# Centring the key weights on VectorE and GpSimd, and placing the first stage's filler work by order

## The chip, the cores and the metric

The kernel runs on one core of a Trainium2 chip. A core has a matrix engine (TensorE, PE in the profile; its weight loads are listed apart as PEld), three engines for elementwise work (VectorE or DVE, ScalarE or ACT, GpSimd or POOL) and a queue that starts transfers from memory (SyncE or SP). Each engine works through its own list of instructions in order, and waits where an operand isn't there yet. The metric is the device time of one execution in microseconds (us); lower is better.

## The reference: what is computed

A transformer block on a query sequence x of 128 rows and 512 columns, with a context of 12,544 rows and 512 columns. Everything is float32.

1. x is normalised twice, and gives self-attention queries q, keys k and values v, and cross-attention queries qx. Before each projection the input is divided by a scale per column, rounded to an 8-bit float, and multiplied back. q, k and qx are normalised per head of 128 columns.
2. The context is projected by `w_kv_x` to keys kx (8 heads of 128) and values vx (8 heads of 128); kx is normalised per head:

```python
kvx = jnp.einsum('bsi,oi->bso', cond, w_kv_x)
kx, vx = jnp.split(kvx, 2, axis=-1)
kx = _ln(kx.reshape(b, sc, g, d), kxln_w, kxln_b)
xout = _gqa(qx, kx, vx)
```

3. Self-attention over the 128 rows (called core) and cross-attention over the 12,544 context rows are concatenated, rounded to 8 bits, projected and added to x.
4. A causal self-attention block and a mixture-of-experts layer follow.

The normalisation of kx subtracts the mean over the 128 columns of a head. As the projection is linear, this mean can be taken from the weights beforehand: if the 128 weights of a head and an input row have their mean subtracted, the keys come out centred. Only the division by the standard deviation is left for later.

## The kernel before, in words

**First stage** (`pre` pools, lines 407 to 618). x is loaded and normalised, and turned (transposed on TensorE). Twelve projections of 512 columns follow: four for qx (numbers 0 to 3), two for k (4, 5), two for v (6, 7), four for q (8 to 11). `begin` (line 456) issues the four matmuls of one projection and asks for a further block of weights by `load_ahead`; `end` (line 475) normalises its result. `norm_heads` (line 147) does that: statistics on DVE (bn_stats, bn_aggr; tile `mv`), three small steps on POOL for the reciprocal deviation (tile `rs`, lines 157 to 160), one on DVE for the shift (tile `nb4b`, line 162), four scalings on ACT (tile `pnn`, line 164). The result is transposed on TensorE (tile `ps_t`) and evicted by ACT (tiles `qraw`, `kT`, `qT`; line 472). The loop at line 516 ends projection i and begins projection i + 3. `quantised` (line 442) makes the rounded inputs on DVE. Sixteen narrow matmuls (`ps_b`, line 536) multiply each head's `qraw` by a bias column. Then four rounds of self-attention, `weights_of` and `heads_of`, end each with a product `ps_core` (line 606), which is added to `x1c`.

**Context products.** Keys and values of a chunk of 512 context rows are computed as a two by two block product with seven block multiplications in place of eight. `mix_tokens` (line 252) makes the mixed input blocks (tiles `mix`), `mix_weights` (line 275) the mixed weight blocks (tiles `wsum`, and parts of `wkv` in place). `unit` (line 287) is a generator with four steps that issue seven products (tiles `a_ps`, `b_ps`, `c_ps`), evicted by ACT (tiles `p`, `u`) and DVE (into `KT` and `V`). `k_unit` gives keys (matmul at line 327), `v_unit` values (matmul at line 346). A chunk needs two units of each, 56 matmuls of 256 columns for the keys and 28 of 512 columns for the values.

**Filler.** The values of chunk 0 don't depend on the centring, so their units are used as work for TensorE between the projections: `filler` holds the eight steps of both value units; `next(filler)` is written at two places of the loop's program text, and the rest is drained after the self-attention, where the scheduler places each matmul by what it finds free. The two key units of chunk 0 follow.

**Centring of the key weights** (lines 545 to 558). For each of the eight blocks of 512 columns (4 row blocks k, 2 halves h) and each of the four heads in it, ACT copies the 128 columns with the scale -1/128 and an accumulated sum (line 555, into `junk`, the sum into `wm`), and then adds that sum to the columns (line 558). `mix_weights` for the keys' half follows on DVE.

**Main loop** (line 780): for each of 25 chunks, `scores` per head group (`s_ps`, line 640; evicted by ACT times the keys' reciprocal deviation `krs`, line 645), maxima on DVE, exponentials on ACT, running sums on POOL (`ol`, line 730), `outputs` (`o_ps`, line 738), and between them the values of this chunk and the keys of the next. `mix_tokens` of the next chunk is asked for there, on POOL; the scheduler issues it up to a chunk earlier. `k_rstd` makes `krs` from the sums of squares: a narrow product (`v_ps`), an addition on DVE (`kve`) and a power on POOL (line 382).

**What sets the order.** The kernel is written against a scheduler which lays out each engine's list when the program is built. `tc.issue_after(x)` keeps an instruction from standing before x. The hardware then follows these lists.

Of the kernel before, what the change touches and what calls it, by code (L numbers as in the profile page):

```python
# [21 lines left out]
T = 12544  # L22
NH, G, D = 16, 8, 128
# [22 lines left out]
def block_kernel(  # L46
# [23 lines left out]
    nc = tc.nc  # L70
# [9 lines left out]
    HS = 2 * S  # L80


    colt = keep.tile([P, NCOL], F32, name="colt")
    nc.sync.dma_start(out=colt, in_=cols)
    sc = keep.tile([P, 6], F32, name="sc")
# [9 lines left out]

    def scl(name):
        return sc[:, scn(name)]

    x1c = keep.tile([S, H], F32, name="x1c")
    nc.sync.dma_start(out=x1c, in_=x)  # L100


    ident = keep.tile([P, P], F32, name="ident")
# [43 lines left out]
    def norm_heads(dst, src, sname):  # L147


        st = small.tile([P, 4, 6], F32, tag="st4", name="st4")  # L150
        mv = small.tile([P, 4, 2], F32, tag="mv4", name="mv4")
        for j in range(4):
            nc.vector.bn_stats(st[:, j, :], src[:, j * D : (j + 1) * D])
        for j in range(4):
            nc.vector.bn_aggr(mv[:, j, :], st[:, j, :])
        v = small.tile([P, 4], F32, tag="ve4", name="ve4")
        nc.gpsimd.tensor_scalar(v, mv[:, :, 1], sc2[:, scn(sname)], EPS, ALU.mult, ALU.add)
        r = small.tile([P, 4], F32, tag="rs4", name="rs4")
        nc.gpsimd.tensor_tensor(r, v, mhalf[:, :4], ALU.pow)
        pool = nc.gpsimd.tensor_scalar(r, r, scl(sname), None, ALU.mult)  # L160
        b = small.tile([P, 4], F32, tag="nb4b", name="nb4b")
        dve = nc.vector.scalar_tensor_tensor(b, mv[:, :, 0], -1.0, r, ALU.mult, ALU.mult)
        for j in range(4):
            act = nc.scalar.activation(
                dst[:, j * D : (j + 1) * D], src[:, j * D : (j + 1) * D], AF.Identity,
                bias=b[:, j : j + 1], scale=r[:, j : j + 1],
            )
        return pool.ins, dve.ins, act.ins

    def norm_rows(dst, src, twice=False):  # L170

# [217 lines left out]
    def parts(units):  # L389
        for u in units:  # L390
            yield from u

    def keys(c, others, pool, tag):

        sums = {}
        todo = parts(k_unit(c, u) for u in range(2))
        for i in range(8):
            next(todo)
            if i % 4 == 3:
                sums[i // 4] = k_sums(c, i // 4)  # L400
            if others:
                others(i)
            if i == 6:
                k_rstd(c, 0, sums.pop(0), pool, tag)
        return sums

    with tc.tile_pool(name="pre", bufs=2) as pre, tc.tile_pool(name="pre1", bufs=1) as pre1, tc.tile_pool(
# [86 lines left out]
            return end_norm(i, "wq", "qln_w", "qln_b", qTs[-1])  # L494

        names = ["qx_in"] * 4 + ["k_in"] * 2 + ["v_in"] * 2 + ["q_in"] * 4
        filler = parts(v_unit(0, v) for v in range(2))
        mix_steps = mix_tokens(0, nc.vector)
        xs["qx_in"], made = quantised("qx_in")
        with tc.issue_after(made), tc.issue_after(turned[0]):  # L500
# [15 lines left out]
        for i in range(12):  # L516
            last = end(i)
            if last is not None:
                pooled, normed, act = last
                if i == 1:  # L520
                    scaled = act
            if i < 2:
                for step in steps[i]:
                    step()
# [6 lines left out]
                    xs[nm], _ = quantised(nm)  # L531
            if i + 3 < 12:
                begin(names[i + 3])
            if i == 3:
                for h in range(NH):
                    nc.tensor.matmul(
                        psb[:, h : h + 1], lhsT=qraws[h // 4][:, h % 4, :], rhs=col("kxln_b"),
                        start=True, stop=True,
                    )
                qbw = pre1.tile([32, NH, 4], F32, name="qbw")  # L540
                for k in range(4):
                    nc.vector.tensor_copy(qbw[:, :, k], psb[32 * k : 32 * k + 32])
                for b in range(4):
                    nc.vector.tensor_copy(qb[32 * b : 32 * b + 32], qbw)
            if i == 7:


                for k in range(NK):
                    for h in range(2):
                        wm = small.tile([P, 4], F32, tag="wm", name="wm", bufs=8)  # L550
                        for g in range(4):
                            wk = wkv[:, k, h, g * D : (g + 1) * D]
                            junk = pre.tile([P, D], F32, tag="junk", name="junk", bufs=1)
                            with tc.issue_after(scaled):
                                nc.scalar.activation(
                                    junk, wk, AF.Copy, scale=-1.0 / D, accum_out=wm[:, g : g + 1]
                                )
                            nc.scalar.activation(wk, wk, AF.Identity, bias=wm[:, g : g + 1])
                for k in range(2):
                    for step in mix_weights(nc.vector, slice(0, H), k):  # L560
                        step()
        made = pooled

        def weights_of(i):
# [48 lines left out]
            heads_of(i, pe)  # L613
            pe = nxt

        for _ in filler:
            pass
        sums = keys(0, None, pps, "ps")

# [5 lines left out]
    with main:  # L625
# [154 lines left out]
        for c in range(NCH):  # L780
# [328 lines left out]
```

## Time and profile before

| | us |
|---|---|
| median of 3 runs | 2216.09 (2210.39 to 2217.72) |
| the profiled execution | 2217.69 |
| its span | 2215.9 |
| TensorE busy in the span | 2162.0 (98%) |
| DVE, POOL, ACT busy in the span | 1287.5, 1066.5, 919.7 |
| first projection starts | 13.95 |
| projection 8 starts | 56.48 |
| first ps_core starts | 95.63 |
| first s_ps starts | 141.34 |
| third o_ps of chunk 0 starts | 176.25 |

Busy time by stretch of the first stage and of chunk 0, in us:

| stretch | TensorE | DVE | ACT | POOL |
|---|---|---|---|---|
| 28.8 to 56.5 | 25.3 of 27.7 | 19.1 | 23.3 | 6.7 |
| 56.5 to 95.6 | 34.7 of 39.1 | 19.6 | 24.6 | 11.4 |
| 95.6 to 141.3 | 45.7 of 45.7 | 23.6 | 11.7 | 0.1 |
| 141.3 to 176.3 | 31.7 of 35.0 | 25.8 | 20.3 | 18.0 |

How to read the lines that follow: a row of the timeline has the start, the length, the engine, the line of the kernel, the operation, the tile written and the tiles read, the shape, and how many instructions were merged; in brackets stands how long the engine was idle before, and what ended that. A matmul in float32 appears as two records, so x8 is four matmuls. DVE is VectorE, ACT is ScalarE, POOL is GpSimd. The granted clock is TensorE's, 1.00 being full speed.

### The profile page before, as it was taken

Reading aid. Unit: us, or ns where it says so; the run is one execution under the profiler, and the core shown is the slowest. Engines: PE = TensorE matmul, PEld = TensorE weight load, DVE = VectorE, ACT = ScalarE, POOL = GpSimd, SP = SyncE. Lnnn points to the kernel's source line nnn. Section 1 sums busy time; section 2 is a strip of 40 time slices with the busy share of each in tenths; the row PEclk is TensorE's granted clock in tenths of the full one; section 3 lists DMA queues with packets and bytes.
Section 4 is the critical chain, followed back from the end, with each engine's and each line's share of the span. In section 5 each row is a group of like instructions: output and inputs, shape, how many; then the busy total and the mean of one; then the engine's idle time right before and its main releaser. Section 6 shows DMA issues by size and latency. Waiting matters only on the chain.

```text
span 2215.9 us, 23861 instructions
## 1 busy us (share of the span) xinstructions
PE 2162.0 (98%) x8660; PEld 1543.1 (70%) x8660; DVE 1287.5 (58%) x2394; ACT 919.7 (42%) x1782; POOL 1066.5 (48%) x1157
## 2 busy tenths in 40 slices
PE   8999999999999999999899999999999999997899
PEld 4477767776776777677676776677677767765554
DVE  7455675566567556656666567556755765674211
ACT  4544454444345434544344444434544443440111
POOL 2214654674475456446574476456546744650000
PEclk9999999999999999999999999999999999998799
DMA  8300000000000000000000000000000000026393
GB/s 309 114 20 1 20 19 1 20 20 19 1 20 20 1 20 20 10 1 20 19 20 20 1 20 19 1 20 20 19 1 20 20 18 2 1 100 233 114 285 118
DMA packets 71222, 95.49 MB, mean 43 GB/s; under 512 B 3136, under 2 KB 39488, under 8 KB 71104
## 3 DMA queue, kind: packets, MB, share of 16 engines
q1 hardware_dynamic: 71104, 93.97, 12.7%
q8 instruction: 68, 1.11, 0.2%
q14 instruction: 50, 0.41, 0.1%
HBM read 93.69 MB, written 0.26 MB: 42 GB/s over the span
## 4 chain that ended last, share of the span: by engine, by line
PE 89%; DVE 4%; POOL 2%; issue 2%; DMA 1%; ACT 1%; SPq 1%; POOLq 0%; ACTq 0%; DVEq 0%
PE a_ps L327 15%; PE o_ps L738 14%; PE s_ps L640 14%; PE a_ps L346 14%; PE c_ps L327 7%; PE c_ps L346 7%; PE gu_ps L1024 4%; PE b_ps L327 4%; PE b_ps L346 4%; PE moe_acc L1045 2%; PE ps_core L606 1%; DVE s L716 1%; DMA w<-in_wqxT 1%; POOL ol L730 1%; PE ps_qk L910 0%
## 5 line engine op out<-in xcount | busy, mean ns | idle before, releaser
L730 POOL TENSOR_TENSOR ol<-ol,s 128x256 f32<-128x256 f32 x764 | 551.9, 731 | 31.2
L645 ACT ACTIVATE s<-s_ps,krs 128x256 f32<-128x256 f32 x784 | 323.2, 470 | 187.4 <-PE s_ps L640 181.5
L382 POOL TENSOR_TENSOR krs<-kve,mhalf 128x16 f32<-128x16 f32 (+1 forms) x50 | 142.9, 2857 | 526.8 <-DVE kve L380 526.8
L722 POOL TENSOR_TENSOR ol<-ol,al 128x512 f32<-128x512 f32 x192 | 243.2, 1278 | 295.5 <-DVE al L699 295.5
L640 PE MATMUL s_ps<-qxT,KT 128*128 128x256 f32 x1568 | 374.8, 382 | 3.3 <-ACT s L645 3.3
L738 PE MATMUL o_ps<-s,V 128*128 128x256 f32 x1568 | 371.5, 379 | 1.8 <-DVE V L316 1.8
L640 PEld LDWEIGHTS s_ps<-qxT,KT 128*128 128x128 f32 x1568 | 296.8, 191 | 104.9 <-issue 67.2
L651 DVE TRANSPOSE_TENSOR_REDUCE mxr<-s 128x32 f32<-128x1024 f32 (+1 forms) x200 | 242.7, 1214 | 185.5 <-ACT s L645 182.6
L738 PEld LDWEIGHTS o_ps<-s,V 128*128 128x128 f32 x1568 | 296.8, 190 | 42.8 <-DVE V L316 2.6
L720 ACT ACTIVATE s<-s 128x1024 f32<-128x1024 f32 (+1 forms) x200 | 207.9, 1040 | 151.3 <-DVE s L716 147.7
L716 DVE TENSOR_TENSOR s<-s,b_ps 128x1024 f32<-128x1024 f32 (+1 forms) x200 | 231.1, 1167 | 0.0
L297 ACT COPY u<-a_ps 128x512 f32<-128x512 f32 (+1 forms) x198 | 114.1, 576 | 254.0 <-PE a_ps L327 208.0
L327 PE MATMUL a_ps<-ctx,wkv 128*128 128x256 f32 (+1 forms) x800 | 186.6, 375 | 0.6 <-POOL ol L722 0.6
L346 PE MATMUL a_ps<-wkv,ctx 128*128 128x512 f32 x392 | 186.2, 597 | 0.0
L743 DVE TENSOR_TENSOR ol<-ol,o_ps 128x256 f32<-128x256 f32 x192 | 79.8, 416 | 176.1 <-PE o_ps L738 165.0
L327 PEld LDWEIGHTS a_ps<-ctx,wkv 128*128 128x128 f32 x800 | 150.0, 190 | 31.1 <-issue 12.4
L363 DVE TRANSPOSE_TENSOR_REDUCE sqr<-sq 128x16 f32<-128x512 f32 (+1 forms) x200 | 128.0, 678 | 58.6 <-ACT sq L361 58.6
L361 ACT ACTIVATE sq<-KT 128x1024 f32<-128x1024 f32 (+1 forms) x100 | 103.9, 1039 | 129.1 <-DVE KT L316 88.2
L316 DVE TENSOR_TENSOR KT<-c_ps,u 128x512 f32<-128x512 f32 (+1 forms) x50 | 34.0, 680 | 144.9 <-PE c_ps L327 144.9
L346 PEld LDWEIGHTS a_ps<-wkv,ctx 128*128 128x128 f32 x392 | 74.8, 192 | 52.8 <-issue 47.9
L327 PE MATMUL a_ps<-mix,wkv 128*128 128x256 f32 (+1 forms) x400 | 97.3, 386 | 7.0 <-ACT u L297 7.0
L327 PE MATMUL c_ps<-ctx,wsum 128*128 128x256 f32 (+1 forms) x400 | 92.9, 375 | 1.1 <-DVE KT L311 1.1
(213 smaller groups left out, 2787.6 us busy)
## 6 DMA issues: line engine op xcount, KB each, us to landing
ctx<-in_ctxT SPq DMA_DIRECT2D x23, 1024.0 KB, 5.0
gu<-in_w SPq DMA_DIRECT2D x32, 384.0 KB, 4.9
gu<-in_v SPq DMA_DIRECT2D x32, 384.0 KB, 5.5
dn<-in_w SPq DMA_DIRECT2D x16, 768.0 KB, 5.7
w<-in_wprojT SPq DMA_DIRECT2D x8, 1024.0 KB, 5.6
w<-in_wqxT SPq DMA_DIRECT2D x4, 1024.0 KB, 9.4
w<-in_wqT SPq DMA_DIRECT2D x4, 1024.0 KB, 4.9
wkv<-in_wkvT SPq DMA_DIRECT2D x8, 256.0 KB, 7.2
```

The source lines that it names most:

```text
L327: nc.tensor.matmul(ps[:, j * h : (j + 1) * h], lhsT=w[:, k, (2 * u + j) * D : (2 * u + j + 1) * D], rhs=x[:, k, :], start=first and j == k ...
L346: last_mm[0] = nc.tensor.matmul(ps, lhsT=x[:, k, v * P : (v + 1) * P], rhs=w[:, k, H : 2 * H], start=first and k == 0, stop=k == 1, skip_g ...
L363: nc.vector.tensor_reduce(r[:, 2 * j + i, : n // 32], sq[:, i, :n].rearrange("p (b i) -> p b i", i=32), AX.X, ALU.add, apply_transpose=True,)
L382: nc.gpsimd.tensor_tensor(rs[:, :, :nt], ve[:, :, :nt], mhalf.rearrange("p (g t) -> p g t", g=4)[:, :, :nt], ALU.pow,)
L640: nc.tensor.matmul(ps[:, t - t0, :], lhsT=KT[:, g, t * P : (t + 1) * P], rhs=qxT[:, 2 * g : 2 * g + 2, :], start=True, stop=True,)
L645: nc.scalar.activation(s[:, t, :], ps[:, t - t0, :], AF.Copy, scale=rs[:, t : t + 1])
L651: nc.vector.tensor_reduce(mxr[g // 4][:, g % 4, :nt, :].rearrange("p t k -> p (t k)"), s[:, :nt, :].rearrange("p t (k i) -> p (t k) i", i=32),
L716: nc.vector.tensor_tensor(s[:, :nt, :], s[:, :nt, :], ps[:, a, None, :].to_broadcast([P, nt, HS]), ALU.subtract,)
L720: nc.scalar.activation(s[:, :nt, :], s[:, :nt, :], AF.Exp, scale=scale)
L722: nc.gpsimd.tensor_tensor(ol[g], ol[g], alb[:, a, None, :].to_broadcast([P, 2, HS]), ALU.mult)
L730: nc.gpsimd.tensor_tensor(ol[g][:, 1, :], first, s[:, t, :], ALU.add)
L738: end = nc.tensor.matmul(ps, lhsT=V[:, t, g * D : (g + 1) * D], rhs=s[:, t, :], start=t == 0, stop=t == nt - 1,)
```

## The change

Five things are changed, all of them in the first stage or in what it hands to chunk 0.

- The load of x is issued first, ahead of two small loads.
- The centring goes from ACT to two other engines. DVE sums the 128 columns of four heads in one reduction per block and scales the sums by -1/128; POOL adds them to the block in one instruction with the sum broadcast over the columns. The eight blocks are spread over rounds 3, 4 and 5 of the loop, each POOL addition behind that round's last POOL step of `norm_heads`.
- `filler` holds only the first value unit of chunk 0. Its steps 3 and 4 are asked for in rounds 2 and 6, behind projections 5 and 9.
- The first step of the first key unit is asked for in round 8, behind projection 11; `keys` takes the generator over with one step done.
- The second value unit of chunk 0 is left to chunk 0 itself, where its steps are taken between the scores as in all other chunks.

```diff
+    x1c = keep.tile([S, H], F32, name="x1c")
+    nc.sync.dma_start(out=x1c, in_=x)
     colt = keep.tile([P, NCOL], F32, name="colt")
     nc.sync.dma_start(out=colt, in_=cols)
...
-    x1c = keep.tile([S, H], F32, name="x1c")
-    nc.sync.dma_start(out=x1c, in_=x)
...
-    def keys(c, others, pool, tag):
+    def keys(c, others, pool, tag, todo=None, done=0):
 
         sums = {}
-        todo = parts(k_unit(c, u) for u in range(2))
-        for i in range(8):
+        todo = todo or parts(k_unit(c, u) for u in range(2))
+        for i in range(done, 8):
...
-        filler = parts(v_unit(0, v) for v in range(2))
+        filler = v_unit(0, 0)
...
             if i + 3 < 12:
                 begin(names[i + 3])
+            if i in (2, 6):
+                with tc.issue_after(begun[i + 3][1]):
+                    next(filler)
...
+            for j in {3: (0,), 4: (1,), 5: range(2, 8)}.get(i, ()):
+                wk = wkv[:, j % 4, j // 4, :H].rearrange("p (g d) -> p g d", g=4)
+                wm = small.tile([P, 4], F32, tag="wm", name="wm", bufs=8)
+                nc.vector.tensor_reduce(wm, wk, AX.X, ALU.add)
+                nc.vector.tensor_scalar(wm, wm, -1.0 / D, None, ALU.mult)
+                with tc.issue_after(pooled):
+                    nc.gpsimd.tensor_tensor(
+                        wk, wk, wm[:, :, None].to_broadcast([P, 4, D]), ALU.add
+                    )
             if i == 7:
-                for k in range(NK):
-                    for h in range(2):
-                        wm = small.tile([P, 4], F32, tag="wm", name="wm", bufs=8)
-                        for g in range(4):
-                            wk = wkv[:, k, h, g * D : (g + 1) * D]
-                            junk = pre.tile([P, D], F32, tag="junk", name="junk", bufs=1)
-                            with tc.issue_after(scaled):
-                                nc.scalar.activation(
-                                    junk, wk, AF.Copy, scale=-1.0 / D, accum_out=wm[:, g : g + 1]
-                                )
-                            nc.scalar.activation(wk, wk, AF.Identity, bias=wm[:, g : g + 1])
                 for k in range(2):
                     for step in mix_weights(nc.vector, slice(0, H), k):
                         step()
+            if i == 8:
+                first_keys = parts(k_unit(0, u) for u in range(2))
+                with tc.issue_after(begun[11][1]):
+                    next(first_keys)
...
-        for _ in filler:
-            pass
-        sums = keys(0, None, pps, "ps")
+        sums = keys(0, None, pps, "ps", first_keys, 1)
...
-            todo = parts(v_unit(c, v) for v in range(chunks[c][1] // HS if c else 0))
+            todo = parts(v_unit(c, v) for v in range(0 if c else 1, chunks[c][1] // HS))
```

In the sections that follow, the twelve projections are numbered as above; norm i is the normalisation of projection i, and "step 3" of a unit is the third of its four steps.

More of the change, by code (lines that the diff above doesn't have):

```diff
@@ L163, in norm_heads @@
         for j in range(4):
-            act = nc.scalar.activation(
+            nc.scalar.activation(
                 dst[:, j * D : (j + 1) * D], src[:, j * D : (j + 1) * D], AF.Identity,
@@ L167, in norm_heads @@
             )
-        return pool.ins, dve.ins, act.ins
+        return pool.ins, dve.ins
     def norm_rows(dst, src, twice=False):
@@ L518, in block_kernel @@
             if last is not None:
-                pooled, normed, act = last
-                if i == 1:
-                    scaled = act
+                pooled, normed = last
             if i < 2:
```

## The prediction

> **What bounds the kernel now.** I read the page first, then the busy time by stage, then the list of what TensorE waited for in the first 180 us, then the timeline of that stretch. The page says that the kernel is a TensorE kernel.
>
> ```profile
> span 2215.9 us, 23861 instructions
> ...
> PE 2162.0 (98%) x8660; PEld 1543.1 (70%) x8660; DVE 1287.5 (58%) x2394; ACT 919.7 (42%) x1782; POOL 1066.5 (48%) x1157
> ...
> PE 89%; DVE 4%; POOL 2%; issue 2%; DMA 1%; ACT 1%; SPq 1%; POOLq 0%; ACTq 0%; DVEq 0%
> ```
>
> So only time in which TensorE stands, or runs at a lower clock, can be won. The waits of TensorE in the first 180 us (who waited for whom, total, times, longest):
>
> ```profile
> PE ps_t L223 <- DVE xn L185: 7.2, 1, 7.2
> PE ps_t L223 <- ACT pnn L164: 6.2, 6, 1.8
> PE s_ps L640 <- ACT s L645: 3.3, 1, 3.3
> PE ps_p L460 <- ACT qraw L472: 0.6, 1, 0.6
> PE ps_p L460 <- DMA w<-in_wqxT: 0.4, 1, 0.4
> ```
>
> The timeline shows where they lie. Columns: start, length, engine, line, operation, tiles, shape, count, and the idle time before.
>
> ```profile
> 21.42 3.70 PE L460 MATMUL ps_p<-w,x_qx_in 128*128 128x512 f32 x8 [0.44 <-DMA w<-in_wqxT]
> ...
> 44.57 0.65 PE L223 MATMUL ps_t<-ident,pnn 128*128 128x128 f32 x4 [1.80 <-ACT pnn L164]
> ...
> 56.48 10.47 PE L460 MATMUL ps_p<-w,x_q_in 128*128 128x512 f32 x24
> ...
> 70.12 5.30 PE L460 MATMUL ps_p<-w,x_q_in 128*128 128x512 f32 x8
> ...
> 159.35 6.27 PE L640 MATMUL s_ps<-qxT,KT 128*128 128x256 f32 x20 [3.27 <-ACT s L645]
> ```
>
> The 5.30 at 70.12 is the same work that took 3.60 at 52.42: after a halt the granted clock falls to half. Busy time by stretch, with the granted clock third from the end:
>
> ```profile
> 71.00:74.00 3.00, 3.00 (x5) 1.31 (x4) 2.71 (x11) 1.46 (x4) 0.19 (x1) 0.50 0.19 72
> ...
> 160.00:163.00 3.00, 3.00 (x8) 2.36 (x7) 2.87 (x6) 1.75 (x6) 0.00 (x0) 0.50 0.00 0
> ```
>
> By single microseconds the half clock holds from 71.0 to 74.4, 81.4 to 84.6 and 159.7 to 163.1: 10.0 us, so 5.0 us lost. I number the twelve projections 0 to 11. After projection 8 starts (56.48) TensorE stands 1.08+0.60+0.31+0.54+1.83+3.27 = 7.6 us. With the clock, 12.6 us can be won there. Between 28.8 and 56.5 it stands only 2.4 us.
>
> **The change part by part.** The instruction order of the built program (it carries no times) shows where each step lands.
>
> *Load of x first.* Its issue moves from 1.62 to 0.72, past two small loads. The gain at the first transposes lies between 0 and 0.9. I take 0: projection 2 starts at 21.42, when its weights land, and the DMA engines are full until then.
>
> *Centring leaves ACT.* 32 groups of 0.30+0.19+0.40 (rows L555, L558) = 28.5 us of ACT go. That frees the pnn and qraw evictions from queueing; it is the gain behind the waits on pnn above.
>
> *Centring on DVE.* Eight reductions of 128x512 to 128x4. Nearest row: L573, 0.69, the same shape out of PSUM. Below: 0.545 (L185, 512 elements, no reduction); above: 1.24 (L651, 1024 elements). I take 0.69, and 0.16 (nb4b, 128x4) for the scaling, 6.8 us in all. They stand between the statistics on DVE's queue, so they delay the norms.
>
> *Centring on POOL.* Eight additions of 128x512 with a per-row operand. Nearest row: L722, 1.28, 128x512 with a broadcast operand. Below: 0.69 (DVE's addition); above: 2.9 (krs, a power). I take 1.28. The first, second and third come right behind the last POOL step of norms 3, 4 and 5, which releases nb4b on DVE. The trace has one such place:
>
> ```profile
> 78.71 1.26 POOL L265 TENSOR_TENSOR mix<-ctx 128x512 f32<-128x512 f32 x1
> 78.78 1.21 DVE L162 SCALAR_TENSOR_TENSOR nb4b<-mv,rs 128x4 f32<-128x4 f32 x1 [1.91 <-POOL rs L160]
> ```
>
> nb4b has a median of 0.162, and ends here with the POOL step. I price 1.05 for each of the three; bounds 0 and 1.05. [...]
>
> *The early bias products (ps_b).* They now stand as groups of eight on TensorE's queue: heads 4 to 7 wait for qraw 1 ahead of projection 4. ACT makes pnn 2 before qraw 1. nb4b 2 came at 35.12 and its DVE queue is unchanged so far, pnn 2 is done at 36.7, qraw 1 (0.77) at 37.5. TensorE gets there at 33.5 and stands 4.0 us, with the values' step 3 and projection 4 behind it, which before filled this time.
>
> *The norm chain, 3 to 5.* nb4b 2 to the end of statistics 3 took 5.8 (35.12 to 40.91). Add two reductions and scalings, 1.7: 42.6. POOL's three steps: 1.9 (40.91 to 42.82), 44.5; held, 45.7. Statistics 4 and qxT: 1.6, 47.3; +1.9 +1.2 = 50.4. nb4b 4 to statistics 5: 5.8 as before (46.20 to 51.98), plus a reduction and scaling 0.85, plus an eviction to V that moved in, 0.65: 57.7; +1.9 +1.2 = 60.8. From nb4b 5's end to projection 8: 2.4 as before (54.05 to 56.48), so **63.3 instead of 56.48: 6.8 us lost**. The 4.0 us halt and a half clock after it lie inside this; TensorE reaches the transposes of norm 5 at 58 to 59.5 and waits. With the bounds of the reduction (three on the path: -0.4 to +1.6) this is 6.4 to 8.4, and 3.6 unheld.
>
> *Keys' weights ready.* Five additions of 1.27 follow nb4b 5, with DVE steps between: 68. The eight L281-L284 steps (start to start 0.61) end at 72.8, statistics 8 at 74.0, its pnn at 77.5. TensorE has projections 8, 9, 10 (3.45 each) and the values' step 4 (3.44) before it needs that: 77.1. Wait 0.4 at most. Were this cover gone, every further us of POOL would be paid.
>
> *From projection 8 to the outputs of the first chunk.* Fillers of 13 us now come by order between the norms: the keys' first step (3.44) covers norms 9 and 10. I count what is left: 0.6 before norm 11's transposes and 0.4 for its held nb4b, 0.2 at ps_o, 0.45 before the second and fourth ps_core, and in the chunk 0.5 at the fourth s_ps tile (krs 2.9 after v_ps against 1.7+2.6 us of matmuls) and 0.7 at the next a_ps (its copy on ACT is behind two exponentials). Sum 3.0 with the 0.2 above. The 3.27 wait goes, because both krs now stand ahead of the mixing of chunk 2 on POOL (before: mixing 150.5 to 155.5, krs to 158.4). A half clock after the halt at 63: 1.7, of which 0.9 lies in waits already counted: 0.8.
>
> *Second half of the values in chunk 0.* The same matmuls, moved behind the keys; cost 0, as TensorE does them somewhere. They take the place of chunk 1's first products in s_ps.
>
> *DMAs.* Weight loads 7 and on are issued when an earlier projection ends, some 4 to 7 us later; their landing takes 4.9 and they are needed 10 us after: 0. The load of chunk 1 goes behind load 8; it is used only at 80.
>
> **Sum**, against the profiled execution (2217.7, span 2215.9): -12.6 + 6.8 + 3.0 + 0.8 = **-2.0 us**, 2215.7. The median of the runs is 1.6 lower: **2214.1 us**. Later stages keep their order.
>
> **Rivals.**
> 1. *nb4b isn't held* (and projection 8 starts at 60.1). Three times 1.05 is back, and the halt before it shrinks under 1 us, so the 0.8 goes too: 6.0 us won, **2210.1**. For it: nine of ten nb4b took 0.16. Against: on those POOL had nothing to start.
> 2. *POOL's additions are dearer*, as the operand steps by group and not by element, which no row has. At twice 1.28: nb4b 3 to 5 end 3.8 later, projection 8 starts at 67.1, the additions end at 77.4, the last seven weight steps at 81.8, pnn 8 at 86.6; projection 11 starts at 86.9, not 77.8, and at half clock (1.7): 10.5 us, **2224.6**. It decides from 1.95 us on, where 3 x 0.67 eats the 2.0 us. Against: every POOL two-input row has 1.27 to 1.46 per 512 elements.
> 3. *The clock.* The halts of 1.80+0.59 at 42.8 left it at 1.00, those at 67 to 70, 78.8 and 156 halved it. If neither new halt does: 0.8 won, **2213.3**; if the new halts are cut in more pieces and both tell in full, 1.7+0.9 more, 2216.7. [...] The trace has the 3.2 to 3.4 us of half clock, but halves also after 1.8 us of standing.
>
> **How the numbers follow.** Forecast with rival 3 in it: 0.55. Rival 1: 0.20. Rival 2: 0.13. Something else: 0.12. 0.3% is 6.6 us, about what a measurement here tells from no change (the runs before lie 7.3 apart): faster means under 2209.4. Faster: half of rival 1, 0.07 of the first, 0.05 of the rest: 0.22. Slower: 0.12 of rival 2, 0.03, 0.05: 0.20. Same: 0.58. The range takes in rival 1 with 3 us of spread below, 2207, and half-dear additions (1.28 to 1.9, projections 2 us later) with spread above, 2221.
>
> **What would show it.** Right: a wait of about 4 us for qraw before projection 4 (36 to 38); projection 8 at 62 to 65; nb4b three times near 1.2; no wait for pnn between 64 and 82 over 1 us; the 3.3 us wait at s_ps gone; the first chunk's third o_ps some 2 us earlier than 176.25. Wrong: projection 8 before 61 (nb4b free, or reductions cheaper); L553 of the new kernel over 1.9 us; a halt for pnn 8 near 77; a new wait in the chunk's outputs behind DVE, which was 98% busy from 160 to 180.

## The result and the profile after

The changed kernel takes 2211.95 us (median of 22 runs, 2210.43 to 2215.83), the kernel before 2216.92 us (22 runs, 2210.39 to 2220.32): a ratio of 0.9981, with a 95% interval from 0.9974 to 0.9987 (the two medians alone give 0.9978). In the medians that is 5.0 us less, and within the 0.3% that the prediction called no change. Forecast were 2.0 us less (2214.1 us, range 2207 to 2221). The profiled execution took 2211.34 us, 6.3 us less than the one before.

The page of the changed kernel gives the same picture of the whole: span, busy time by engine, the chain that ended last.

```profile
span 2209.6 us, 23790 instructions
...
PE 2160.6 (98%) x8660; PEld 1543.5 (70%) x8660; DVE 1298.2 (59%) x2410; ACT 899.2 (41%) x1686; POOL 1074.5 (49%) x1165
...
PE 90%; DVE 4%; POOL 1%; ACT 1%; SPq 1%; DMA 1%; issue 1%; POOLq 0%; ACTq 0%; DVEq 0%
```

ACT has 20.5 us less to do, DVE 10.7 and POOL 8.0 more. What TensorE waited for in the first 185 us (total, times, longest):

```profile
PE ps_t L222 <- DVE xn L184: 7.2, 1, 7.2
PE ps_b L536 <- ACT qraw L471: 3.6, 1, 3.6
PE a_ps L326 <- ACT u L296: 3.1, 1, 3.1
PE ps_p L459 <- DMA w<-in_wqxT: 0.8, 1, 0.8
PE ps_t L222 <- ACT pnn L163: 0.5, 1, 0.5
```

The 6.2 us for pnn have shrunk to 0.5 and the 3.3 us at s_ps are gone. New are 3.6 us for qraw and 3.1 us for ACT's copy u. TensorE's timeline shows where (start, length, engine, line, operation, tiles, shape, count, idle time before):

```profile
21.50 3.70 PE L459 MATMUL ps_p<-w,x_qx_in 128*128 128x512 f32 x8 [0.77 <-DMA w<-in_wqxT]
...
37.33 1.87 PE L536 MATMUL ps_b<-colt,qraw 128*128 128x1 f32 x8 [3.60 <-ACT qraw L471]
39.06 5.50 PE L459 MATMUL ps_p<-w,x_k_in 128*128 128x512 f32 x8
...
60.25 1.02 PE L222 MATMUL ps_t<-ident,pnn 128*128 128x128 f32 x3 [0.51 <-ACT pnn L163]
61.11 7.04 PE L459 MATMUL ps_p<-w,x_q_in 128*128 128x512 f32 x16
...
171.84 3.17 PE L326 MATMUL a_ps<-mix,wkv 128*128 128x256 f32 x8 [3.13 <-ACT u L296]
```

Projection 8 starts at 61.11 (56.48 before), and from there no wait of TensorE is longer than 0.1 us until 168.7. The granted clock, third from the end, is halved in two places, from 35.9, inside the new halt for qraw, and from 172.4, behind the one for u, and no longer at 71 to 74 or 160 to 163 (1.00 in both):

```profile
36.00:42.60 6.60, 5.27 (x12) 3.22 (x13) 6.10 (x23) 1.28 (x3) 0.96 (x2) 0.50 0.14 55
172.50:175.80 3.30, 3.30 (x10) 2.55 (x9) 2.23 (x4) 1.96 (x4) 3.06 (x5) 0.50 0.03 5
71.00:74.00 3.00, 3.00 (x9) 1.33 (x8) 1.25 (x9) 1.82 (x5) 1.45 (x4) 1.00 0.52 194
```

After 190 us the two kernels do the same work. A halt of 7.05 us in the middle chunk serves as a mark. Before it ended at 1074.40:

```profile
1074.40 3.70 PE L327 MATMUL a_ps<-mix,wkv 128*128 128x256 f32 x8 [7.05 <-ACT u L297]
```

and after at 1068.60, 5.8 us earlier:

```profile
1068.60 3.75 PE L326 MATMUL a_ps<-mix,wkv 128*128 128x256 f32 x8 [7.06 <-ACT u L296]
```

So the gain was made in the first 190 us. By 190 us TensorE has started 26 more records of 128x256, which follow each other at 0.216 us: 5.6 us, nearly the whole 5.8. The mark, the start of the matmul behind this halt, is used below too. It shows what an edit did in the profiled execution before the rest of the program adds its own spread: from the mark to the end of the span every kernel does the same, and that took 1140.4 to 1144.0 us.

### The profile page after: what moved, and what is told of

The parts are those of the page before. It is cut to its first block, busy times and chain, and to the rows that moved or that the text cites. A ratio compares the mean times of both kernels' runs of the same rounds, so it can differ in the third digit from the quotient of the medians.

```text
span 2209.6 us, 23790 instructions
## 1 busy us (share of the span) xinstructions
PE 2160.6 (98%) x8660; PEld 1543.5 (70%) x8660; DVE 1298.2 (59%) x2410; ACT 899.2 (41%) x1686; POOL 1074.5 (49%) x1165
## 4 chain that ended last, share of the span: by engine, by line
PE 90%; DVE 4%; POOL 1%; ACT 1%; SPq 1%; DMA 1%; issue 1%; POOLq 0%; ACTq 0%; DVEq 0%
PE a_ps L326 15%; PE s_ps L640 14%; PE o_ps L738 14%; PE a_ps L345 14%; PE c_ps L326 7%; PE c_ps L345 7%; PE gu_ps L1024 4%; PE b_ps L326 4%; PE b_ps L345 4%; PE moe_acc L1045 2%; PE ps_p L459 1%; PE ps_core L608 1%; DVE s L716 1%; DMA w<-in_wqxT 1%; POOL ol L730 1%
## 5 line engine op out<-in xcount | busy, mean ns | idle before, releaser
L730 POOL TENSOR_TENSOR ol<-ol,s 128x256 f32<-128x256 f32 x764 | 551.8, 730 | 31.2
```

What stands on the lines that cost most here:

```text
L730: nc.gpsimd.tensor_tensor(ol[g][:, 1, :], first, s[:, t, :], ALU.add)
```

## The experiments

The theory going in: the norms' chain through DVE and POOL sets when projection 8 starts, TensorE's halt for qraw lies inside it, and freeing ACT is what took the waits for pnn away. Ratios are against the kernel before, with 95% intervals; medians in us. Since the weights of projection 2 land at 21.2 to 22.0, projection 8 is given as its distance from the start of projection 3: 27.65 us before, 32.20 in the changed kernel. This distance also moves by itself: nb4b 2, which stands ahead of all the edits, ends 5.0 to 6.5 us after the start of projection 3 (6.1 in the changed kernel). So where it matters, the distance from the end of nb4b 2 to projection 8 is given as well: 21.2 us before, 26.1 in the changed kernel. "At the mark" compares the start of that matmul with 1068.60 of the changed kernel.

**Bias products later.** Edit on the changed kernel:

```diff
             if i == 3:
-                for h in range(NH):
-                    nc.tensor.matmul(psb[:, h : h + 1], ...)
+                with tc.issue_after(begun[6][1]):
+                    for h in range(NH):
+                        nc.tensor.matmul(psb[:, h : h + 1], ...)
```

> The 32 products of the query bias (ps_b) are ordered behind projection 6; nothing else changes, and nothing is left out. Theory A (the one on record: the norms' chain through DVE and POOL sets when projection 8 starts, and the 3.6 us halt before projection 4 lies inside its slack): the halt goes, projection 4 starts near 33.7 instead of 39.06, but statistics 4 waited only 0.24 us for TensorE, so projection 8 starts at 60.5 to 61.1 (61.11 in the changed kernel), TensorE stands some 6 us before the transposes of norms 4 and 5 instead, and the time is 2211 to 2212 us. Theory B (the halt and its half clock set it, since TensorE reaches norm 5's transposes at 59.47, only 0.5 us ahead of their data): projection 8 starts at 56 to 58 and the time is 2207 to 2209 us.

2213.16 us, ratio 0.9986 (0.9977 to 0.9995): no faster than the changed kernel. TensorE's timeline:

```profile
33.39 3.67 PE L459 MATMUL ps_p<-w,x_k_in 128*128 128x512 f32 x8
...
45.27 1.52 PE L222 MATMUL ps_t<-ident,pnn 128*128 128x128 f32 x4 [2.62 <-ACT qraw L471]
...
60.51 7.04 PE L459 MATMUL ps_p<-w,x_q_in 128*128 128x512 f32 x16
```

Projection 4 starts 5.7 us earlier, projection 8 at a distance of 31.2, only 1.0 less, and from nb4b 2 it is 25.9 us, 0.2 less. TensorE waits in another place, 2.6 us and not some 6, with a half clock period there (the four transposes took 1.52 us, 0.60 elsewhere). Theory A holds: the halt was inside the slack of the chain. The time came out a microsecond above its range; at the mark this execution is 0.5 us ahead.

**Additions with no fixed place.** This was meant to put POOL's additions behind nb4b of the same norm, and no longer behind POOL's last step of it, so that none runs beside nb4b; nothing is left out.

```diff
-                with tc.issue_after(pooled):
+                with tc.issue_after(normed):
                     nc.gpsimd.tensor_tensor(wk, wk, ..., ALU.add)
```

> [...] Theory A (holding nb4b is on the chain): nb4b 3, 4 and 5 take 0.16 instead of 0.99 and end at about 43.5, 47.7 and 56.1 instead of 44.36, 49.33 and 58.62. TensorE, still halted and slowed before projection 4, reaches norm 5's transposes at 59.5, so projection 8 starts at 60.0 instead of 61.11, and the time falls by 1.1 us, to about 2211. Rival: nb4b is held for another reason, or it isn't on the chain: the rows stay near 0.99, or projection 8 stays at 61.1, and the time at 2212.

2209.29 us, ratio 0.9973 (0.9963 to 0.9983). The order that came out isn't the one intended: the edge to DVE's nb4b left POOL free, and additions came to stand between POOL's steps of a norm. POOL's timeline, and nb4b 3 on DVE:

```profile
41.33 0.27 POOL L156 TENSOR_SCALAR ve<-mv,sc 128x4 f32<-128x4 f32 x1 [4.05 <-DVE wm L551]
41.55 1.04 POOL L553 TENSOR_TENSOR wkv<-wkv,wm 128x512 f32<-128x512 f32 x1
42.55 1.03 POOL L158 TENSOR_TENSOR rs<-ve,mhalf 128x4 f32<-128x4 f32 x1
...
44.02 0.16 DVE L161 SCALAR_TENSOR_TENSOR nb4b<-mv,rs 128x4 f32<-128x4 f32 x1 [1.55 <-POOL rs L159]
```

nb4b is held no more (0.16, not 0.99), but the addition now costs the chain its 1.0 us inside POOL: nb4b 3 ends 10.4 us after nb4b 2, against 9.4. So this run doesn't price the hold. Five additions are done before nb4b 5, not two, so the last ends at 61.25, not 63.6. Projection 8 is at 30.4, 1.8 less, but 1.0 of this was there at nb4b 2, before any addition; from nb4b 2 it is 25.4 us, 0.7 less. The interval overlaps that of the changed kernel.

**Both edits.** The two diffs above together.

> The two edits together: bias products behind projection 6, additions behind nb4b. If the chain and the halt are two paths of nearly one length (60.2 and 59.5), each alone brings 0 to 1.1 us, but both together bring the whole 2.5 us of the three held nb4b: projection 8 at 58.0 to 58.6 and the time 2209 to 2209.5. If the chain alone counts, it is the same as the additions alone by the rows (60.0 or 58.6); if the halt alone counts, the same as the bias products alone.

2211.76 us, ratio 0.9979 (0.9970 to 0.9988); projection 8 at 32.1. The expectation failed, and this run can't add the two up, as the second edit wasn't what it said. It shows a loss that none had counted. Busy time by stretch, TensorE first, granted clock third from the end:

```profile
53.50:56.80 3.30, 3.30 (x25) 2.82 (x26) 2.68 (x12) 0.32 (x1) 1.20 (x2) 1.00 0.85 309
56.90:60.20 3.30, 3.30 (x6) 1.24 (x5) 2.64 (x10) 2.17 (x5) 2.73 (x5) 0.50 0.00 0
```

TensorE is busy without a gap in the first stretch, but largely with bias products of 128x1, and in the next its clock is halved.

**The values' second half back in the first stage.**

```diff
-        filler = v_unit(0, 0)
+        filler = parts(v_unit(0, v) for v in range(2))
...
-                first_keys = parts(k_unit(0, u) for u in range(2))
                 with tc.issue_after(begun[11][1]):
-                    next(first_keys)
+                    next(filler)
...
-        sums = keys(0, None, pps, "ps", first_keys, 1)
+        for _ in filler:
+            pass
+        sums = keys(0, None, pps, "ps")
...
-            todo = parts(v_unit(c, v) for v in range(0 if c else 1, chunks[c][1] // HS))
+            todo = parts(v_unit(c, v) for v in range(chunks[c][1] // HS if c else 0))
```

> The second half of the first chunk's values goes back into the first stage (its first step takes the place of the keys' first step behind projection 11, the others stand ahead of the keys). Theory A (the 3.27 us wait of the kernel before at s_ps came from the second krs standing behind the mixing of chunk 2 on POOL, and it went because the keys now come before it): the wait is back, 3 to 3.5 us near 157, with half clock after it, and the 3.13 us wait at a_ps near 172, which the fuller chunk 0 brought, is gone or under 1.5 us; the time stays within 1.5 us of 2212. Rival (the wait went because ACT no longer centres, or the fillers' order): no wait at s_ps over 1 us, and the time falls to about 2207 to 2209.

2212.72 us, ratio 0.9982 (0.9973 to 0.9991). The second krs is behind the mixing on POOL again, and the wait at s_ps is back. First POOL, then TensorE:

```profile
148.79 1.27 POOL L267 TENSOR_TENSOR mix<-ctx,mix 128x512 f32<-128x512 f32 x1
150.02 2.91 POOL L381 TENSOR_TENSOR krs<-kve,mhalf 128x16 f32<-128x16 f32 x1
...
153.86 6.08 PE L641 MATMUL s_ps<-qxT,KT 128*128 128x256 f32 x20 [3.32 <-ACT s L646]
175.94 1.99 PE L326 MATMUL c_ps<-ctx,wsum 128*128 128x256 f32 x8 [1.32 <-DVE KT L310]
```

The 3.13 us at a_ps are gone, 1.32 for DVE have come. Theory A holds: this part of the change took one wait of 3.3 us away and brought another of 3.1, and is worth nothing.

**Centring back on ACT.** With this edit the kernel is the one before with the other four parts of the change.

```diff
-            for j in {3: (0,), 4: (1,), 5: range(2, 8)}.get(i, ()):
-                wk = wkv[:, j % 4, j // 4, :H].rearrange("p (g d) -> p g d", g=4)
...
             if i == 7:
+                for k in range(NK):
+                    for h in range(2):
+                        wm = small.tile([P, 4], F32, tag="wm", name="wm", bufs=8)
+                        for g in range(4):
...
+                            with tc.issue_after(scaled):
+                                nc.scalar.activation(
+                                    junk, wk, AF.Copy, scale=-1.0 / D, accum_out=wm[:, g : g + 1]
+                                )
+                            nc.scalar.activation(wk, wk, AF.Identity, bias=wm[:, g : g + 1])
```

> The centring of the keys' weights goes back to ACT, after projection 7's step as in the kernel before; the order of the fillers, the place of the values and the load of x stay as changed. Theory A (the waits for pnn between 64 and 82 came from ACT's 28.5 us of centring; the additions and reductions cost the norms' chain 4.6 us): nb4b 3 to 5 are free again and the chain ends some 5 us earlier, so that projection 8 is set by TensorE's own halt before projection 4, at 59 to 60 instead of 61.1; but waits for pnn of 3 to 5 us come back between 64 and 84, with one or two half clock periods of 1.7 us: 2214 to 2218 us. Rival (the fillers' order alone covers those waits): no wait for pnn over 1 us between 64 and 84, and the time is 2209 to 2211 us.

2212.87 us, ratio 0.9985 (0.9975 to 0.9995): the intervals don't tell it from the changed kernel; at the mark this execution is 2.2 us behind. Theory A failed: TensorE's only wait for pnn in the first 190 us is 0.7 us. The rival's time was missed too, because the halt for qraw, with ACT busy again, now sets projection 8 (distance 32.4):

```profile
39.41 1.87 PE L538 MATMUL ps_b<-colt,qraw 128*128 128x1 f32 x8 [5.22 <-ACT qraw L471]
...
61.77 7.03 PE L459 MATMUL ps_p<-w,x_q_in 128*128 128x512 f32 x16
86.28 0.68 PE L222 MATMUL ps_t<-ident,pnn 128*128 128x128 f32 x2 [0.68 <-ACT pnn L163]
```

So the work put between them is enough to cover norms 8 to 11; a free ACT isn't needed for that.

**Keys' first step not put early.**

```diff
-            if i == 8:
-                first_keys = parts(k_unit(0, u) for u in range(2))
-                with tc.issue_after(begun[11][1]):
-                    next(first_keys)
...
-        sums = keys(0, None, pps, "ps", first_keys, 1)
+        sums = keys(0, None, pps, "ps")
```

> The keys' first step is no longer put behind projection 11; all steps of the keys come after the first stage, where the scheduler places them. Theory A (that step's 3.44 us cover norms 9 and 10): TensorE is done with projection 11 at about 78.7 and then waits for pnn of norms 10 and 11 (ready near 80.5 and 84.5): 2 to 4 us of waits between 78 and 85, likely with one half clock period of 1.7 us, so 2214 to 2217 us. Rival (the scheduler finds other work, or the waits only move): under 1 us of waits there and 2212 us.

2215.52 us, ratio 0.9997 (0.9988 to 1.0007): no gain is left that the runs show. TensorE waits 1.4 us for pnn behind projection 11, in two pieces (another 1.0 us lies at norm 5, where the changed kernel waits 0.5), and the chunk's outputs wait in another place:

```profile
83.71 0.68 PE L222 MATMUL ps_t<-ident,pnn 128*128 128x128 f32 x2 [1.13 <-ACT pnn L163]
...
175.13 1.97 PE L326 MATMUL a_ps<-mix,wkv 128*128 128x256 f32 x8 [2.02 <-POOL ol L726]
```

Theory A holds for the time and the place, but the waits are shorter than its 2 to 4 us and no half clock follows them (the products behind the wait for ol took 1.97 us, those of a_ps behind the halt of the changed kernel, where it does follow, 3.17). At the mark this execution is 1.6 us behind the changed kernel, less than the 3.6 us of the medians; what makes the rest isn't shown. This step is the only part whose undoing moves the time beyond the intervals, and it does so barely (0.9988 against 0.9987).

**Copy u ahead of the exponentials.** In the first chunk's outputs only; copied[0] is the last copy that unit() made.

```diff
             for a in range(2):
...
-                nc.scalar.activation(s[:, :nt, :], s[:, :nt, :], AF.Exp, scale=scale)
+                with tc.issue_after(behind) if behind else nullcontext():
+                    nc.scalar.activation(s[:, :nt, :], s[:, :nt, :], AF.Exp, scale=scale)
...
-                if i in (5, 6, 9, 10):
+                if c == 0 and i in (10, 11):
+                    spread(c, i - 8, copied[0])
+                elif i in (5, 6, 9, 10) and (c or i < 9):
                     spread(c, i // 4 * 2 - 2 + (i - 1) % 4)
```

> In the outputs of the first chunk, ACT's exponentials of key groups 4 to 7 are ordered behind the copy u of the next chunk's keys. Theory A (the 3.13 us wait at a_ps near 172 is that copy standing behind an exponential that waits for DVE): the copy runs at about 167 instead of 171.1 and the wait for ACT u goes; the following c_ps then waits for DVE's KT (172.6, behind two subtractions) for 1.5 to 2.2 us, in two smaller halts instead of one, perhaps without the half clock after it: 1 to 3 us won, 2209 to 2211 us. Rival (DVE sets the pace of this stretch): the wait only moves to c_ps or o_ps with its whole length, and the time stays at 2212 us.

2209.13 us, ratio 0.9968 (0.9958 to 0.9979). In the changed kernel the copy is behind an exponential (ACT):

```profile
170.17 1.06 ACT L720 ACTIVATE s<-s 128x1024 f32<-128x1024 f32 x1 [6.20 <-DVE s L716]
171.13 0.57 ACT L296 COPY u<-a_ps 128x512 f32<-128x512 f32 x1
```

and here it is ahead of it (ACT, then TensorE):

```profile
166.95 0.59 ACT L296 COPY u<-a_ps 128x512 f32<-128x512 f32 x1 [3.03 <-PE a_ps L326]
170.11 1.06 ACT L721 ACTIVATE s<-s 128x1024 f32<-128x1024 f32 x1 [2.58 <-DVE s L716]
...
172.13 1.99 PE L326 MATMUL c_ps<-ctx,wsum 128*128 128x256 f32 x8 [1.76 <-DVE KT L310]
```

Theory A holds in place and size: 3.13 us became 1.76, and no half clock follows (the products behind the wait took 1.99 us, 3.17 in the changed kernel). The interval touches that of the changed kernel, but at the mark this execution is 3.1 us ahead.

**All additions behind norm 5.**

```diff
-            for j in {3: (0,), 4: (1,), 5: range(2, 8)}.get(i, ()):
+            for j in range(8) if i == 5 else ():
...
-                nc.vector.tensor_scalar(wm, wm, -1.0 / D, None, ALU.mult)
+                with tc.issue_after(normed):
+                    nc.vector.tensor_scalar(wm, wm, -1.0 / D, None, ALU.mult)
```

> All eight additions of POOL stand behind POOL's last step of norm 5, and the scalings that they read are ordered behind nb4b 5 on DVE, so that no nb4b between norms 3 and 5 has an addition beside it and no addition stands between POOL's steps of a norm. Theory A (each held nb4b costs the chain 0.83 us): nb4b 3, 4, 5 take 0.16; from nb4b 2's end to nb4b 5's end it is 21.1 us instead of 23.6, TensorE (halted before projection 4) reaches norm 5's transposes first, and projection 8 starts 31.2 us after projection 3 instead of 32.2. The additions end near 65.5 instead of 63.6, still ahead of the norms that need the weights. Time 2210.5 to 2211.5 us. Rival (the chain isn't what sets projection 8, or POOL's later end is paid by the keys): projection 8 stays 32.2 after projection 3, or a wait over 1 us appears between 64 and 84, and the time is 2212 or more.

2214.97 us, ratio 0.9990 (0.9980 to 0.9999). This is the test that the second run missed. All three nb4b take 0.16, and nb4b 5 ends 22.2 us after nb4b 2 (23.6 in the changed kernel); projection 8 is at 30.1, 2.1 less, or 1.1 less from nb4b 2. But the additions end at 65.4, DVE idles for them, and norm 8 is late (DVE, then TensorE):

```profile
64.45 2.11 DVE L280 TENSOR_TENSOR wsum<-wkv 128x512 f32<-128x512 f32 x2 [4.00 <-POOL wkv L554]
...
74.09 1.38 PE L222 MATMUL ps_t<-ident,pnn 128*128 128x128 f32 x4 [0.91 <-ACT pnn L163]
```

From projection 8 to the first ps_core it takes 39.4 us, 36.5 in the changed kernel. The chain part of theory A holds; in this trace the rival's second half outweighs it: more than projection 8 won is paid at the keys' weights, and at the mark the execution is 2.3 us behind. The intervals overlap, so the runs alone don't show that it is slower.

**Centring on ACT and bias products later.** The diffs of the first and the fifth run together.

> Centring back on ACT, and the bias products behind projection 6. Theory A (the order of the fillers is what took the waits away, and moving the centring off ACT brought nothing of its own: with the centring on ACT the norms' chain is short, and TensorE's halt for qraw is what sets projection 8): without the halt projection 8 starts 27.5 to 29.5 us after projection 3 instead of 32.4, some of it given back in waits of 1 to 3 us between 70 and 86, since ACT's centring ends no earlier; 2209 to 2212 us. Rival (freeing ACT is worth something by itself): the waits for pnn or for the centred weights grow by all that projection 8 gains, and the time stays at 2213 us or above.

2211.86 us, ratio 0.9973 (0.9964 to 0.9982). Without the halt and without the additions projection 8 is at 28.3 (57.27), and 2.1 us of waits for pnn, none over 0.7, and 1.6 us for qraw come instead. Theory A holds. Set beside the bias products later with centring on DVE and POOL (0.9986, 0.9977 to 0.9995), taking the centring off ACT isn't shown to win anything; the intervals overlap, and at the mark the order is the other way round (1069.28 here, 1068.06 there), so it isn't shown to lose either.

**The same with the copy u ahead.** The diff of the run before and that of the seventh.

> The same with ACT's copy u ordered ahead of the exponentials in the first chunk's outputs. That edit brought 2.8 us on the changed kernel; if the two places are independent it brings 2 to 3 us here too: 2206.5 to 2209.5 us. If DVE's lateness in the first chunk's outputs grows when TensorE comes there earlier, under 1 us.

2209.37 us, ratio 0.9966 (0.9954 to 0.9979): 2.5 us less in the medians, as expected for independent places, though the intervals overlap. At the mark this execution is the first of all, at 1063.71, 4.9 us ahead of the changed kernel.

**Additions with no fixed place and copy u ahead.** The diffs of the second and the seventh run together, on the changed kernel.

> On the changed kernel, the two edits that were faster together: POOL's additions without their place behind POOL's last step of a norm, and the copy u ahead of the exponentials. If they are independent: 2.7 + 2.8 us, so 2206 to 2207.5 us. If the first one's gain was a matter of the clock's windows (projection 8 moved only 1.8 us), 2208 to 2209.5 us.

2207.24 us, ratio 0.9961 (0.9948 to 0.9973): the lowest median of all, some 9 us under the kernel before and 4 to 5 under the changed kernel, whose interval (0.9974 to 0.9987) lies just above. In the medians the two edits add up nearly in full, but the traces don't bear that out. At the mark this execution stands at 1065.03, and copy u alone at 1065.53: the additions bring 0.5 us between these two, and from nb4b 2 to projection 8 it is 25.4 us, 0.7 less than in the changed kernel, as in the second run. The interval overlaps those of copy u alone and of the run before, so it isn't shown to be faster than either.

**Additions twice.**

```diff
-                nc.vector.tensor_scalar(wm, wm, -1.0 / D, None, ALU.mult)
+                nc.vector.tensor_scalar(wm, wm, -0.5 / D, None, ALU.mult)
                 with tc.issue_after(pooled):
-                    nc.gpsimd.tensor_tensor(wk, wk, ..., ALU.add)
+                    for _ in range(2):
+                        nc.gpsimd.tensor_tensor(wk, wk, ..., ALU.add)
```

> Every addition on POOL is made twice with half the mean, so each costs 2.0 us instead of 1.0; nothing is left out. Theory A (rival 2 of the prediction: past nb4b 5 each further us of POOL is paid, since the weight steps, statistics 8 and the later norms stand behind it): the last addition ends near 70 instead of 63.6, the weight steps near 76, TensorE waits 3 to 6 us for pnn 8 to 10 and loses one or two half clock periods: 2216 to 2220 us. Rival (covered by projections 8 to 10): waits under 1 us between 70 and 85, and 2212 to 2213 us.

2217.86 us, ratio 1.0009 (1.0000 to 1.0018): 5.9 us above the changed kernel, and 5.9 behind it at the mark. POOL, then TensorE:

```profile
57.52 12.00 POOL L554 TENSOR_TENSOR wkv<-wkv,wm 128x512 f32<-128x512 f32 x12
...
78.20 1.52 PE L222 MATMUL ps_t<-ident,pnn 128*128 128x128 f32 x4 [3.22 <-ACT pnn L163]
```

Six more microseconds of POOL behind nb4b 5 cost six. Theory A holds.

## Why the prediction was right or wrong

That the change makes no difference beyond 0.3% was right, and so was the kind of sum: what TensorE loses between projection 8 and the second chunk, against what the norms' chain adds. The size was 3 us off in the medians and 3.8 at the mark. Point by point:

- *x first, taken at 0*: right. The first transposes wait 7.2 us in both, and projection 2 waits for its weights until 21.50 (21.42).
- *Reductions 0.69, scaling 0.16*: right. The tile wm has reductions of 0.656 to 0.683, the scaling a median of 0.158.
- *Additions 1.28*: too dear. All eight take 1.04, and six in a row take 6.02. Their operand steps by group, and they came cheaper than the rows of 128x512 that the sum went by (1.25 to 1.28), not dearer.
- *Three nb4b held by 1.05*: right in number and nearly in size. The timeline has them with the additions:

```profile
43.30 1.04 POOL L553 TENSOR_TENSOR wkv<-wkv,wm 128x512 f32<-128x512 f32 x1
43.37 0.99 DVE L161 SCALAR_TENSOR_TENSOR nb4b<-mv,rs 128x4 f32<-128x4 f32 x1 [1.27 <-POOL rs L159]
...
57.57 6.02 POOL L553 TENSOR_TENSOR wkv<-wkv,wm 128x512 f32<-128x512 f32 x6
57.63 0.99 DVE L161 SCALAR_TENSOR_TENSOR nb4b<-mv,rs 128x4 f32<-128x4 f32 x1 [1.28 <-POOL rs L159]
```

  Each ends with the first POOL addition beside it, at 44.36 and 58.62. The one such place in the trace before, 1.21 us beside a POOL step of 1.26, had shown the same. Rival 1, an nb4b that isn't held, is out.
- *TensorE stands 4.0 us for qraw, at no cost*: right (3.60). Taking the halt away isn't shown to win anything (0.9986); with the centring on ACT, where the chain is short, the halt does set projection 8.
- *The chain costs 6.8 us*: mis-sized; 4.6 measured (61.11, not 63.3). Statistics 3 end at 41.46, not 42.6: I added reductions and scalings in full to the old distance, but part of them fills gaps between dependent DVE steps (qz_y to the next step is 0.46 start to start before, where that step needs its result, and 0.33 after, where a scaling stands there). The same holds at norm 5, where only 0.8 us came of the 1.5 added to the old distance. The three holds are shorter by 0.2 each, and against that statistics 4 end 0.5 later than priced, 0.24 of it in a wait for TensorE.
- *Keys' weights in time, wait at most 0.4*: right, no wait. That every further microsecond behind nb4b 5 would be paid was borne out: six more cost six. The 1.95 us per addition from which rival 2 was to decide isn't tested by that run: it rested on three longer holds, and there nb4b 3 to 5 still took 0.99.
- *Waits left after projection 8, 3.0 us in all*: the sum was right, 3.1, but by accident. The five in the first stage and at s_ps, 2.15 us with ps_o, didn't come. The one at a_ps, 0.7, came as 3.13: its cause was named (the copy behind exponentials), but the exponential itself waited for DVE's subtraction until 170.1, and I hadn't followed DVE's queue through that stretch.
- *0.8 us of half clock after projection 8's halt*: it didn't come: that halt was 0.5, and the clock behind it stayed at 1.00. The 3.13 us halt brought 1.8 us instead (3.17 + 2.41 against 1.89 twice).
- *12.6 us won*: right, and 1.1 more, as the wait of c_ps for KT at 181.42, which I had left standing, went too.
- *The markers*: the third o_ps, forecast 2 us earlier, is at 166.82, since the order around it changed; it was no measure of time. Projection 8 at 61.11 lies under the 62 to 65 that was to show the forecast right. And one sign of being wrong came: the wait at a_ps goes back to an exponential behind DVE.

That the total came so near is luck in part: the chain was 2.2 us too dear and 1.1 us of gain was left out, while 1.0 us of half clock was missing on the other side. With the measured terms: -12.6 - 1.1 + 4.6 + 3.1 + 1.8 = -4.2, against -5.8 at the mark. The remaining 1.6 us lie in no row of a wait but in TensorE's busy time. Up to the mark both kernels have the same 4254 matmul records, and with the half clock taken off they keep TensorE busy for 1.7 us less after the change. 0.8 us of this is in the transposes, which before were issued singly between waits (0.33 each, where four together take 0.60); the rest is spread over the products.

The reason given for the gain is the step that doesn't hold. The prediction put the waits for pnn down to ACT's centring ("it is the gain behind the waits on pnn above") and treated the order of the fillers as cover beside it. The runs show that the fillers are enough. With the centring back on ACT, which is the kernel before with the other four parts, one wait of 0.7 us for pnn is left and the kernel is faster than before (0.9985, 0.9975 to 0.9995). At the mark these four parts bring 3.6 of the 5.8 us. The other 2.2 come with the centring on DVE and POOL, 1.4 of them between projection 8 and the first ps_core. Without the keys' first step behind projection 11, 1.4 us of these waits come back, and the median rises by 3.6 us. Whether a free ACT alone would have been enough too stays open: the centring alone, moved in the kernel before with its old fillers, wasn't tried.

## What to carry to other kernels

When TensorE is the bound, work placed by order between dependent steps can hide a late engine as well as relieving that engine does. Both had a price here: the relief lengthened the norms' chain by 4.9 us, and the new order brought TensorE a halt for qraw, which set projection 8 until the bias products were moved too (32.4 and 28.3 us with the centring on ACT). Before pricing a wait as gone, follow the queue of the engine behind it to the next instruction that waits: here a 3.3 us wait left one place and a 3.1 us wait arose in another. And where two paths end together, undo each alone and both: a halt that costs nothing now may be what sets the time once the other path is short. Where the rest of a program has a spread of its own, compare the traces at a mark right behind the change as well as by medians.

## What the runs showed of the hardware

- The half clock comes in periods of 3.41 us, alone or several in a row (two after, from 35.91 to 42.74; five before, from 2050.71 to 2067.77), on a grid that runs through a whole trace. Before, the periods start at 71.00, 81.20 and 159.70, which is 3 and 23 steps of 3.41 apart; after, at 35.90 and 172.45, 40 steps apart. The clock granted in them is 0.50, so that each lost at most 1.7 us. What seems to decide is how long TensorE works in one window of the grid, that is in the 3.41 us between two of its steps. Between 20 and 1100 us of the fourteen traces, windows at full clock in which TensorE was busy for 1.57 us or less were all followed by half clock, windows with 1.61 to 2.4 us mostly not (1.61 and 1.92 kept it; 2.01, 2.03 and 2.17 didn't). Before, the windows from 77.80 (1.56 us busy) and 67.56 (2.01) were followed by half clock, and that from 43.67 (1.92) wasn't; after, those from 32.50 (1.24) and 169.03 (0.60) were, and that from 1059.91 (1.63) wasn't. So a halt of 1.8 us may bring no half clock (1.80 at 42.8 before, 1.76 at 170.4 with the copy u ahead) or a period that costs 1.7 us more (1.83 at 78.8 before), by where it falls.
- Products of 128x1 seem to count for little: four windows were busy for their whole 3.41 us, but more than half of that with them. Where the wider products in them came to 0.85 us (centring on ACT with copy u ahead) and 1.36 us (both edits), half clock followed; where they came to 1.39 us (centring on ACT and bias products later) and 1.49 us (bias products later), it didn't.
- The grid lies elsewhere in each execution (its first step is 2.71 us into the span before and 1.78 in the changed kernel), and that moves the time of work that nobody touched. Between 1960 and 2100 us every kernel does the same; TensorE's busy time there, times what the granted clock lacked (in steps of 0.5 us), comes to 16.1 to 16.7 us in nine of the fourteen profiled executions (16.4 before, 16.6 in the changed kernel) and to 17.6 to 19.5 in the other five, 18.7 with the bias products later and 19.3 with the additions in no fixed place. The profiled execution of the latter took 2212.5 us, its median is 2209.3. From the mark to the end of the span ten executions take 1140.4 to 1141.5 us and four take 1143.8 to 1144.0 (bias products later, additions in no fixed place, keys' first step not put early, centring on ACT with copy u ahead). In these four the mark lies 0.9 to 1.1 us behind a step of the grid, in the other ten 0.6 or at least 1.3. A profile alone doesn't settle a few microseconds of this kernel.
- Two other DVE steps were longer beside an addition on POOL too: with one running, qz_y took 0.90 us and qz_e 0.76 (second run, and the same where that edit ran with the copy u ahead), without 0.42 and 0.28.
